# The last forty LSTM steps: kept input parts copied into PSUM by ScalarE, gates in three banks, order by hand

## The chip, the cores and the metric

One core of a Trainium2 chip runs the whole layer. The metric is the device time of one execution in microseconds (us), the median of three runs. The engines are named as in the profile: PE is TensorE's matmuls, PEld its weight loads, ACT is ScalarE, DVE is VectorE, POOL is GpSimd, SP the queue that issues DMAs.

## The reference, cut to what matters

A graph layer (6250 nodes, 256 features, 100000 edges) adds a gather-and-sum network and a linear attention block to x. Its result goes through a layer norm and then an LSTM over all 6250 nodes as one sequence, a gate by argmax and weighted prefix and suffix sums. The change is in the LSTM:

```python
x_proj = einsum('btd,gd->btg', x, W_ih) + b_ih + b_hh
def step(carry, xp):
    h, c = carry
    gates = xp + h @ W_hh.T
    i, f, g, o = split(gates, 4)
    c = sigmoid(f) * c + sigmoid(i) * tanh(g)
    h = sigmoid(o) * tanh(c)
...
logits = lstm_out @ W_lin.T + b_lin
w = argmax(logits) * lstm_out          # two classes: 0 or 1
inc = cumsum(w)
return 2 * lstm_out + (inc - w) * fw_att + (inc[-1] - inc) * bw_att
```

## The kernel before, in words

The sequence of 6250 is cut into NC = 125 pieces of NS = 50 nodes, which run side by side: one column per piece. A piece needs the state at the end of the piece before it. The kernel gets it by a warm-up: every piece first runs its own last WARM = 40 steps from a zero state, and the state reached is handed to the next piece as its beginning (line 984). Then all 50 steps run for good. At the end the final states are compared with those that had been handed on, to a tolerance of 2^-20 (lines 1011 to 1023); only if one differs by more does a loop node by node run instead (line 1028 on). So the loop at line 980 has 90 steps: 40 warm ones (s = 10 to 49), then s = 0 to 49.

State and gates lie with features on the partitions: h and c are two halves (a = 0, 1) of 128 partitions x 125 columns, and each half's four gates are four blocks of 125 columns in one PSUM bank. A step (`step`, line 938) adds W_hh's products onto banks that already hold the inputs' products: for each half a, gate g and half k of h one matmul, 16 in all (line 945). Then, half by half, ACT makes the four gates with the bias in the instruction (line 954), DVE i*g, f*c and their sum c (lines 960 to 962), ACT tanh(c) (line 964) and DVE h (line 965). While that runs, PE brings the inputs of the next step into the other pair of banks.

There are two ways in which they come. In the warm steps and for s = 0 to 9, `inputs` (line 905) multiplies the normed rows by W_ih: 16 matmuls (line 912). In the warm steps `store` (line 917) also copies these banks to SBUF, bank 0 by ACT (line 920) and bank 1 by DVE (line 921), and sends them to HBM (line 922). In the last forty steps, whose inputs are the same as in the warm ones, `fetch` (line 924) gets them back, two steps ahead of use, and `inputs_again` (line 929) puts them into PSUM by one matmul of 500 columns with the identity for each half (line 933). In these steps the products of h go by k first (`by_half`), so that the first eight need only h's first half.

Beside the steps run `residual`, `normed`, `columns` and `kept`, which prepare the normed rows of later steps, and `gated` (line 832) for the step before: two matmuls of h with w_d give the difference of the logits on all partitions (line 835), DVE masks h with it into w (line 837), adds w to inc (line 842), and adds w and inc to h, each with a weight per feature, half by half (line 845): four instructions. `gated` writes h in place, so it comes after the products that read it.

The order on each engine is set by a scheduler at compile time, from the program's order and the dependencies; two instructions on one PSUM bank of a tile are kept in order.

Of the kernel before, what the change touches and what calls it, by code (L numbers as in the profile page):

```python
# [26 lines left out]

NC, NS = 125, 50
HEADS, HC = 8, 32
KD = D // P  # L30
# [23 lines left out]
BANK = 512  # L54
# [6 lines left out]
WARM = 40  # L61
# [15 lines left out]
def gps_layer(ctx: ExitStack, tc: tile.TileContext, x, src, dst, cols, rows, kvln, wqkv, mw1, mw2, gw1, gw2,  # L77
              wih, whh, blstm, out):
    nc = tc.nc
# [4 lines left out]
    x_d = dram.tile([WARM * P, KD * 4 * NC], F32, name="x_d")  # L84


    ident = big.tile([P, P], F32, name="ident")
# [79 lines left out]
    with ExitStack() as s1:  # L167
# [535 lines left out]
        with tc.manual_schedule(engines={mybir.EngineType.PE, mybir.EngineType.DVE, mybir.EngineType.Activation}):  # L703
# [3 lines left out]
            while slot < GROUPS - COUNTED or running or before or any(s >= slot for s in starts):  # L707
                g = slot + COUNTED
# [91 lines left out]
    def block(g, a):  # L800
        return slice((g * KD + a) * P, (g * KD + a + 1) * P)
# [3 lines left out]

    begin_h = wl.tile([P, KD, NC], F32, name="begin_h")
    begin_c = wl.tile([P, KD, NC], F32, name="begin_c")
    c = wl.tile([P, KD, NC], F32, name="c")

# [12 lines left out]
    for k in range(KD):  # L822
        d = wl.tile([P, 1], F32, name="wlin_d")
        nc.vector.tensor_sub(d, col("wlin", 2 * k + 1), col("wlin", 2 * k))
        nc.vector.tensor_scalar(w_d[:, k, :], ones, d, None, op0=ALU.mult)
    one_r = ones[:, :NC]
    inc = wl.tile([P, KD, NC], F32, name="inc")
    rest = wl.tile([P, KD, NC], F32, name="rest")
    rest_t = wl.tile([P, D], F32, name="rest_t")

    def gated(s, pool, pl):

        h_s = hs[:, :, s * NC:(s + 1) * NC]
        for k in range(KD):
            nc.tensor.matmul(pl, w_d[:, k, :], h_s[:, k, :], start=(k == 0), stop=(k == KD - 1))
        w = pool.tile([P, KD, NC], F32, name="w")
        nc.vector.scalar_tensor_tensor(w, pl[:, None, :].to_broadcast([P, KD, NC]), thr, h_s, op0=ALU.is_gt,
                                       op1=ALU.mult)
        if s == 0:
            nc.vector.tensor_copy(inc, w)  # L840
        else:
            nc.vector.tensor_add(inc, inc, w)
        for i, t in ((0, w), (2, inc)):
            for k in range(KD):
                nc.vector.scalar_tensor_tensor(h_s[:, k, :], t[:, k, :], half[:, i, k:k + 1], h_s[:, k, :],
                                               op0=ALU.mult, op1=ALU.add)

    def others(pool, pt):

        for k in range(KD):  # L850
            sums_k = pool.tile([P, NC], F32, name="sums_k")
            nc.vector.tensor_tensor_scan(sums_k, one_r, inc[:, k, :], 0.0, op0=ALU.mult, op1=ALU.add)
            every = pool.tile([P, 1], F32, name="every")
            nc.vector.tensor_mul(every, sums_k[:, NC - 1:NC], half[:, 1, k:k + 1])
            nc.vector.tensor_sub(sums_k, sums_k, inc[:, k, :])
            nc.vector.tensor_scalar(rest[:, k, :], sums_k, half[:, 2, k:k + 1], every, op0=ALU.mult, op1=ALU.add)
            nc.tensor.transpose(pt[:NC, k * P:(k + 1) * P], rest[:, k, :], ident)
        nc.vector.tensor_scalar(rest_t[:NC], pt[:NC], 2.0, None, op0=ALU.mult)

    with tc.tile_pool(name="lstm", bufs=2) as rp, tc.tile_pool(name="ps3", bufs=4, space=PSUM) as ps, \  # L860
            tc.tile_pool(name="ps_y", bufs=2, space=PSUM) as ps_y:

        AHEAD, FETCH = 3, 2

        def residual(s):

# [50 lines left out]
        def store(s, banks):  # L917

            t = rp.tile([P, KD, 4 * NC], F32, name="x_out", bufs=1)
            nc.scalar.copy(t[:, 0, :], banks[0].rearrange("p g c -> p (g c)"))  # L920
            nc.vector.tensor_copy(t[:, 1, :], banks[1].rearrange("p g c -> p (g c)"))
            nc.sync.dma_start(x_d[(s - NS + WARM) * P:(s - NS + WARM + 1) * P, :], t.rearrange("p k m -> p (k m)"))

        def fetch(s):
            t = rp.tile([P, KD, 4 * NC], F32, name="x_in", bufs=FETCH)
            nc.sync.dma_start(t.rearrange("p k m -> p (k m)"), x_d[(s - NS + WARM) * P:(s - NS + WARM + 1) * P, :])
            return t

        def inputs_again(t):
            banks = []  # L930
            for a in range(KD):
                pg = ps.tile([P, 4, NC], F32, name="pg")
                nc.tensor.matmul(pg.rearrange("p g c -> p (g c)"), ident, t[:, a, :], start=True, stop=False,
                                 skip_group_check=True)
                banks.append(pg)
            return banks

        def step(banks, h, put, by_half):


            if h is not None:
                parts = [(k, a) for a in range(KD) for k in range(KD)]
                for k, a in sorted(parts) if by_half else parts:
                    for g in (I, G, F, O):
                        nc.tensor.matmul(banks[a][:, SLOT[g], :], w_hh[:, k, block(g, a)], h[:, k, :], start=False,  # L945
                                         stop=(k == KD - 1), skip_group_check=True)
            for a in range(KD):
                pg = banks[a]
                gate = {}
                for g in (I, G, F, O):  # L950
                    if g == F and h is None:
                        continue
                    gate[g] = rp.tile([P, NC], F32, name=f"gate{g}")
                    nc.scalar.activation(gate[g], pg[:, SLOT[g], :], AF.Tanh if g == G else AF.Sigmoid,  # L954
                                         bias=bias(g, a))
                if h is None:
                    nc.vector.tensor_mul(c[:, a, :], gate[I], gate[G])
                else:
                    new = rp.tile([P, NC], F32, name="new")
                    nc.vector.tensor_mul(new, gate[I], gate[G])  # L960
                    nc.vector.tensor_mul(gate[F], gate[F], c[:, a, :])
                    nc.vector.tensor_add(c[:, a, :], gate[F], new)
                t_c = rp.tile([P, NC], F32, name="t_c")
                nc.scalar.activation(t_c, c[:, a, :], AF.Tanh)
                nc.vector.tensor_mul(put(a), gate[O], t_c)

        order = [(s, True) for s in range(NS - WARM, NS)] + [(s, False) for s in range(NS)]
        minus_half = rp.tile([P, 1], F32, name="minus_half", bufs=1)
        nc.vector.memset(minus_half, -0.5)
        fresh = iter([s for s, _ in order if s >= NS - WARM][:WARM] + list(range(NS - WARM)))  # L970
        first = [residual(next(fresh)) for _ in range(AHEAD)]
        first = [normed(*r) for r in first]
        for r in first:
# [2 lines left out]
        h = None  # L976
        banks = inputs(order[0][0])
        store(order[0][0], banks)
        fetched = {}
        for i, (s, warm) in enumerate(order):  # L980
            if s == 0:
                for t, of in ((begin_h, h), (begin_c, c)):
# [1 line left out]
                    nc.vector.tensor_copy(t[:, :, 1:], of[:, :, :NC - 1])  # L984
                nc.vector.tensor_copy(c, begin_c)
                h = begin_h
            now = rp.tile([P, KD, NC], F32, name="h_w") if warm else hs[:, :, s * NC:(s + 1) * NC]
            step(banks, h, lambda a: now[:, a, :], not warm and s >= NS - WARM)
            for t in at_columns:
                kept(*t)  # L990
            ready = [normed(*t) for t in at_residual]
            if i + 1 < len(order):
                s_next, warm_next = order[i + 1]
                if s_next in fetched:
                    banks = inputs_again(fetched.pop(s_next))
                else:
                    banks = inputs(s_next)
                    if warm_next:
                        store(s_next, banks)
            s_far, warm_far = order[min(i + 1 + FETCH, len(order) - 1)]  # L1000
            if not warm_far and s_far >= NS - WARM and i + 1 + FETCH < len(order):
                fetched[s_far] = fetch(s_far)
# [4 lines left out]
            at_residual = [residual(s) for s in islice(fresh, 2 if i % 5 == 4 else 1)]  # L1007
            h = now


        agree = rp.tile([P, 1], F32, name="agree", bufs=1)
        parts = rp.tile([P, 2], F32, name="parts", bufs=1)
        for i, (end, begin) in enumerate(((h, begin_h), (c, begin_c))):
            d = rp.tile([P, KD, NC - 1], F32, name="d")
# [3 lines left out]
            nc.vector.reduce_sum(parts[:, i:i + 1], d.rearrange("p k c -> p (k c)"), axis=AX.X)  # L1018
        nc.vector.tensor_add(agree, parts[:, 0:1], parts[:, 1:2])
        pa = ps.tile([P, BANK], F32, name="pg")  # L1020
# [3 lines left out]
        gated(NS - 1, rp, ps_y.tile([P, D], F32, name="pm")[:, :NC])  # L1024
        others(rp, ps_y.tile([P, D], F32, name="pm"))
# [128 lines left out]
```

## Time and profile before

| | |
|---|---|
| median of 3 runs | 1652.07 us (1650.72 to 1653.43) |
| the profiled execution | 1649.37 us, span 1646.5 us, mean granted clock of TensorE 0.958 |
| PE busy over the span | 1498.1 us (91%) |
| DVE, ACT, POOL | 947.2 (58%), 611.7 (37%), 695.2 (42%) |
| gather, attention and graph network | to about 960 us |
| warm steps | x_out first at 964.3, last at 1287.6 us |
| last forty steps | first identity matmul at 1368.3, last at 1591.4 us |
| after them | agreement, weighted sums, output, to 1646.5 us |

A stretch of the warm steps, by the same columns as elsewhere in the document (stretch, length, then busy time and number of instructions of PE, PEld, DVE, ACT and POOL, granted clock, DMA share, GB/s):

```profile
1200.00:1300.00 100.00, 100.00 (x847) 100.00 (x846) 57.63 (x221) 49.49 (x158) 7.60 (x14) 1.00 0.14 58
```

How to read it: a float32 matmul shows as two records on PE, each with a weight load. A timeline line gives the start, the length of a run of like instructions, the engine, the line of the kernel, output and inputs, shapes and the number; in brackets stands how long the engine had been idle and what ended that. In lines of groups the number after the bar is the busy time in us and the mean duration in ns, and after the second bar the idle time before them.

### The profile page before, as it was taken

Reading aid. Unit: us, or ns where it says so; the run is one execution under the profiler, and the core shown is the slowest. Engines: PE = TensorE matmul, PEld = TensorE weight load, DVE = VectorE, ACT = ScalarE, POOL = GpSimd, SP = SyncE. Lnnn points to the kernel's source line nnn. Section 1 sums busy time; section 2 is a strip of 40 time slices with the busy share of each in tenths; the row PEclk is TensorE's granted clock in tenths of the full one; section 3 lists DMA queues with packets and bytes.
Section 4 is the critical chain, followed back from the end, with each engine's and each line's share of the span. In section 5 each row is a group of like instructions: output and inputs, shape, how many; then the busy total and the mean of one; then the engine's idle time right before and its main releaser. Section 6 shows DMA issues by size and latency. Waiting matters only on the chain. (4 is left out here: it accounts for less than half of the span.)

```text
span 1646.5 us, 30983 instructions
## 1 busy us (share of the span) xinstructions
PE 1498.1 (91%) x11312; PEld 1398.0 (85%) x11312; DVE 947.2 (58%) x3028; ACT 611.7 (37%) x1866; POOL 695.2 (42%) x713
## 2 busy tenths in 40 slices
PE   1688899899989969999999889999999999999985
PEld 1477788888889969998999879999999998888864
DVE  6878778888842212222222285555555556777777
ACT  2553323433311114333332244555554434444440
POOL 0277777777777747777777400000000000000005
PEclk9689989999989979999999989999999999999996
DMA  9533333333346683333333321111111001333214
GB/s 243 188 89 98 102 101 100 100 100 99 101 142 177 172 196 103 104 106 105 104 106 105 117 74 65 54 60 64 63 64 64 26 1 63 96 94 88 88 51 157
DMA packets 57708, 166.00 MB, mean 101 GB/s; under 512 B 13040, under 2 KB 21879, under 8 KB 55669
## 3 DMA queue, kind: packets, MB, share of 16 engines
q0 software_dynamic: 31008, 84.71, 18.2%
q1 hardware_dynamic: 22884, 75.07, 14.2%
q10 hardware_dynamic: 3652, 4.11, 1.1%
q8 instruction: 93, 1.52, 0.4%
q14 instruction: 71, 0.58, 0.1%
HBM read 130.56 MB, written 33.28 MB: 100 GB/s over the span
## 5 line engine op out<-in xcount | busy, mean ns | idle before, releaser
L380 POOL DMA_INDIRECT eg<-xn_d,si x646 | 643.5, 996 | 220.3 <-issue 99.0
L401 PE MATMUL pg<-here,eg 128*128 128x96 f32 x2584 | 399.5, 281 | 54.7 <-DMA eg<-xn_d,si 40.5
L401 PEld LDWEIGHTS pg<-here,eg 128*128 128x128 f32 x2584 | 363.9, 198 | 86.3 <-DMA eg<-xn_d,si 43.3
L954 ACT ACTIVATE gate<-pg,b_l 128x125 f32<-128x125 f32 x718 | 201.8, 366 | 229.7 <-PE pg L945 228.4
L411 DVE TENSOR_TENSOR sums<-sums,pg 128x192 f32 x162 | 57.4, 354 | 381.9 <-PE pg L401 200.5
L912 PE MATMUL pg<-yT,w_ih 128*128 128x125 f32 x1600 | 186.9, 275 | 0.0
L945 PE MATMUL pg<-sums,w_hh 128*128 128x125 f32 x1568 | 183.1, 275 | 0.0
L912 PEld LDWEIGHTS pg<-yT,w_ih 128*128 128x128 f32 x1600 | 182.7, 192 | 0.1
L945 PEld LDWEIGHTS pg<-sums,w_hh 128*128 128x128 f32 x1568 | 179.0, 192 | 0.0
L881 POOL TENSOR_TENSOR ln_r<-ln_v,minus_half 125x1 f32<-125x1 f32 x50 | 27.4, 552 | 343.1 <-DVE ln_v L879 314.5
L1083 POOL TENSOR_TENSOR xr<-xr,rest_t 125x1024 f32<-125x1024 f32 x8 | 22.9, 2898 | 312.3 <-DVEq L1028 312.3
L945 PE MATMUL pg<-h_w,w_hh 128*128 128x125 f32 x1248 | 146.0, 276 | 0.2 <-ACT x_out L920 0.2
L945 PEld LDWEIGHTS pg<-h_w,w_hh 128*128 128x128 f32 x1248 | 143.1, 192 | 0.6 <-ACT x_out L920 0.4
L620 ACT ACTIVATE sums<-mm,vec 128x125 f32<-128x125 f32 x100 | 36.5, 365 | 269.5 <-DVE sums L411 178.8
L604 PE MATMUL mm<-sums,g 128*128 128x125 f32 x800 | 119.1, 285 | 1.8 <-DVE counts L643 1.6
L615 PE MATMUL mm<-z,g 128*128 128x125 f32 x800 | 114.7, 284 | 1.0 <-ACT z L610 1.0
L604 PEld LDWEIGHTS mm<-sums,g 128*128 128x128 f32 x800 | 106.6, 198 | 5.3 <-issue 1.8
L455 PE MATMUL mm<-m,xnT 128*125 128x256 f32 x400 | 107.9, 394 | 0.6 <-DVE counts L643 0.5
L615 PEld LDWEIGHTS mm<-z,g 128*128 128x128 f32 x800 | 102.0, 196 | 1.1 <-ACT z L610 1.1
L463 ACT ACTIVATE mm<-kv 125x512 f32<-125x512 f32 x50 | 30.1, 602 | 190.7 <-DVE kv L460 190.7
L610 ACT ACTIVATE z<-mm,vec 128x125 f32<-128x125 f32 x200 | 56.3, 367 | 91.5 <-PE mm L604 91.5
L391 DVE TENSOR_TENSOR here<-iota,drel 128x384 f32<-128x384 f32 x162 | 89.3, 551 | 0.0
(239 smaller groups left out, 2162.6 us busy)
## 6 DMA issues: line engine op xcount, KB each, us to landing
x_d<-x_out SPq DMA_DIRECT2D x40, 500.0 KB
x_in<-x_d SPq DMA_DIRECT2D x40, 500.0 KB
xr<-in_x_dram SPq DMA_DIRECT2D x10, 1120.0 KB
eg<-xn_d,si POOLq DMA_INDIRECT x646, 2.8
counts<-xn_d SPq DMA_DIRECT2D x16, 384.0 KB
xn_d<-xn SPq DMA_DIRECT2D x5, 1120.0 KB
out_dram<-o SPq DMA_DIRECT2D x12, 448.0 KB
xr<-in_x_dram SPq DMA_DIRECT2D x10, 130.0 KB
```

Source lines behind the costliest of these rows:

```text
L380: nc.gpsimd.indirect_dma_start(out=g, out_offset=None, in_=xn_d[:], in_offset=bass.IndirectOffsetOnAxis(ap=at, axis=0))
L391: nc.vector.tensor_tensor(here[:, :n, :], iota[:, None, :W].to_broadcast([P, n, W]), drel[:, gi * GT:gi * GT + n, None].to_broadcast([P, n ...
L401: nc.tensor.matmul(pg[:, k, :], g[:, k * P:(k + 1) * P], here[:, i, :], start=(i == 0 and k == 0), stop=(i == n - 1), skip_group_check=True)
L411: nc.vector.tensor_add(window, window, pg)
L455: nc.tensor.matmul(pkv[:r, at], xnT[:, k, j * NC:(j + 1) * NC], w_qkv[:, k, D:][:, at], start=(k == 0 and half == 0), stop=(k == KD - 1), ...
L604: nc.tensor.matmul(p1[:, m, :], g1[:, k, m * P:(m + 1) * P], sums[:, k, at], start=(m == 0 and k == 0), stop=(k == KD - 1), skip_group_che ...
L610: nc.scalar.activation(z1[:, m, :], p1[:, m, :], AF.Relu, bias=col("gb1", m))
L615: nc.tensor.matmul(p2[:, a, :], g2[:, m, a * P:(a + 1) * P], z1[:, m, :], start=(a == 0 and m == 0), stop=(m == 2 * KD - 1), skip_group_ch ...
L620: nc.scalar.activation(sums[:, a, at], p2[:, a, :], AF.Identity, bias=col("gb2", a))
L912: nc.tensor.matmul(pg[:, SLOT[g], :], w_ih[:, k, block(g, a)], yT[:, k, s * NC:(s + 1) * NC], start=(i == 0 and k == 0), stop=False, skip_ ...
L945: nc.tensor.matmul(banks[a][:, SLOT[g], :], w_hh[:, k, block(g, a)], h[:, k, :], start=False, stop=(k == KD - 1), skip_group_check=True)
L954: nc.scalar.activation(gate[g], pg[:, SLOT[g], :], AF.Tanh if g == G else AF.Sigmoid, bias=bias(g, a))
```

## The change

The loop of 90 steps becomes one of 50 (40 warm, then s = 0 to 9). The last forty steps are written out as a part of their own, in an order by hand for PE, DVE and ACT (`manual_schedule`):

- The kept inputs have the biases in them: `store` writes bank + bias, both halves by a DVE add.
- The gates of a step lie in three banks: i, f, o of half 0, the same of half 1, and g of both halves. There are two sets of three.
- The kept inputs of the next step come into the other set by three ScalarE copies (250, 375 and 375 columns). For steps 10 and 11 the identity matmuls do it.
- One tanh makes g of both halves, one sigmoid makes i, f and o of a half, without a bias in the instruction. tanh(g) and c lie side by side (`gc`), so that i*g and f*c are one multiply.
- `gated` is taken apart: logits right behind the step's products on PE, and on DVE the mask, the sum and the weighting by inc behind h; the weighting by w goes into the next step, before each half of h.
- Three fetched inputs are kept instead of two.

In the steps before, the four gates are now one tile, and `new` is made in place. The diff, cut to its core:

```diff
-    c = wl.tile([P, KD, NC], F32, name="c")
+    gc = wl.tile([P, KD, 2, NC], F32, name="gc")
+    c = gc[:, :, 1, :]
+    b_s = wl.tile([P, KD, 4], F32, name="b_s")
+    for g in range(4):
+        nc.vector.tensor_copy(b_s[:, :, SLOT[g]], b_l[:, g * KD:(g + 1) * KD])
...
+    def logits(s, pl):
         for k in range(KD):
-            nc.tensor.matmul(pl, w_d[:, k, :], h_s[:, k, :], start=(k == 0), stop=(k == KD - 1))
+            nc.tensor.matmul(pl, w_d[:, k, :], of_step(s)[:, k, :], start=(k == 0), stop=(k == KD - 1))
+
+    def weighted(s, i, of, k):
+        h_k = of_step(s)[:, k, :]
+        nc.vector.scalar_tensor_tensor(h_k, of[:, k, :], half[:, i, k:k + 1], h_k, op0=ALU.mult, op1=ALU.add)
+
+    def summed(s, pool, pl):
...
+        for k in range(KD):
+            weighted(s, 2, inc, k)
+        return w
...
-        AHEAD, FETCH = 3, 2
+        AHEAD, FETCH = 3, 3
...
-            nc.scalar.copy(t[:, 0, :], banks[0].rearrange("p g c -> p (g c)"))
-            nc.vector.tensor_copy(t[:, 1, :], banks[1].rearrange("p g c -> p (g c)"))
+            for a in range(KD):
+                nc.vector.tensor_tensor(t[:, a, :].rearrange("p (g c) -> p g c", g=4), banks[a],
+                                        b_s[:, a, :, None].to_broadcast([P, 4, NC]), op=ALU.add)
...
-        order = [(s, True) for s in range(NS - WARM, NS)] + [(s, False) for s in range(NS)]
+        KEPT = NS - WARM
+        order = [(s, True) for s in range(KEPT, NS)] + [(s, False) for s in range(KEPT)]
...
+        sets = [([ps.tile([P, 3, NC], F32, name=f"pg{i}{a}") for a in range(KD)], ps.tile([P, KD, NC], F32, name=f"pg_g{i}"))
+                for i in range(2)]
+
+        def into_banks(s, t):
+            others_a, g_b = sets[s % 2]
+            parts = [(g_b, t[:, :, SLOT[G], :])] + [(others_a[a], t[:, a, :SLOT[G], :]) for a in range(KD)]
+            if s < KEPT + 2:
+                return [partial(nc.tensor.matmul, to, ident, of, start=True, stop=False, skip_group_check=True)
+                        for to, of in parts]
+            return [partial(nc.scalar.copy, to, of) for to, of in parts]
...
+        with tc.manual_schedule(engines={mybir.EngineType.PE, mybir.EngineType.DVE, mybir.EngineType.Activation}):
+            for bring in into_banks(KEPT, fetched.pop(0)):
+                bring()
+            fetched.append(fetch(KEPT + FETCH))
+            w = None
+            for s in range(KEPT, NS):
+                more = into_banks(s + 1, fetched.pop(0)) if s + 1 < NS else []
+                for k, a_ifo in ((0, 0), (1, 0), (0, 1), (1, 1)):
+                    gates = [(I, a_ifo), (F, a_ifo), (O, a_ifo)]
+                    for g, a in gates if a_ifo else [(G, a) for a in range(KD)] + gates:
+                        product(s, g, a, k)
+                pl = ps_y.tile([P, BANK], F32, name="pl")[:, :NC]
+                logits(s - 1, pl)
+                others_a, g_b = sets[s % 2]
+                nc.scalar.activation(gc[:, :, 0, :], g_b, AF.Tanh)
+                for a in range(KD):
+                    gates = rp.tile([P, 4, NC], F32, name="gates")[:, :SLOT[G], :]
+                    nc.scalar.activation(gates, others_a[a], AF.Sigmoid)
+                    for bring in more[a:a + 1]:
+                        bring()
+                    two = rp.tile([P, 2, NC], F32, name="two", tag="h_w")
+                    nc.vector.tensor_mul(two, gates[:, :2, :], gc[:, a])
+                    nc.vector.tensor_add(c[:, a, :], two[:, 0, :], two[:, 1, :])
+                    t_c = rp.tile([P, NC], F32, name="t_c")
+                    nc.scalar.activation(t_c, c[:, a, :], AF.Tanh)
+                    if w is not None:
+                        weighted(s - 2, 0, w, a)
+                    nc.vector.tensor_mul(of_step(s)[:, a, :], gates[:, SLOT[O], :], t_c)
+                for bring in more[KD:]:
+                    bring()
+                w = summed(s - 1, rp, pl)
+                if s + 1 + FETCH < NS:
+                    fetched.append(fetch(s + 1 + FETCH))
+            for k in range(KD):
+                weighted(NS - 2, 0, w, k)
```

More of the change, by code (lines that the diff above doesn't have):

```diff
@@ L829, in gps_layer, with of_step @@
     rest_t = wl.tile([P, D], F32, name="rest_t")
-    def gated(s, pool, pl):
-        h_s = hs[:, :, s * NC:(s + 1) * NC]
+    def of_step(s):
+        return hs[:, :, s * NC:(s + 1) * NC]
+    def logits(s, pl):
         for k in range(KD):
-            nc.tensor.matmul(pl, w_d[:, k, :], h_s[:, k, :], start=(k == 0), stop=(k == KD - 1))
+            nc.tensor.matmul(pl, w_d[:, k, :], of_step(s)[:, k, :], start=(k == 0), stop=(k == KD - 1))
[3 more added lines that the diff above has]
+    def summed(s, pool, pl):
         w = pool.tile([P, KD, NC], F32, name="w")
-        nc.vector.scalar_tensor_tensor(w, pl[:, None, :].to_broadcast([P, KD, NC]), thr, h_s, op0=ALU.is_gt,
+        nc.vector.scalar_tensor_tensor(w, pl[:, None, :].to_broadcast([P, KD, NC]), thr, of_step(s), op0=ALU.is_gt,
                                        op1=ALU.mult)
@@ L842, in gated @@
             nc.vector.tensor_add(inc, inc, w)
[L843 to L846, printed above, removed]
+        for k in range(KD):
+            weighted(s, 2, inc, k)
+        return w
+    def gated(s, pool, pl):
+        logits(s, pl)
+        w = summed(s, pool, pl)
+        for k in range(KD):
+            weighted(s, 0, w, k)
     def others(pool, pt):
         for k in range(KD):
-            sums_k = pool.tile([P, NC], F32, name="sums_k")
+            sums_k = pool.tile([P, NC], F32, name="sums_k", tag="t_c")
             nc.vector.tensor_tensor_scan(sums_k, one_r, inc[:, k, :], 0.0, op0=ALU.mult, op1=ALU.add)
@@ L858, in others @@
         nc.vector.tensor_scalar(rest_t[:NC], pt[:NC], 2.0, None, op0=ALU.mult)
-    with tc.tile_pool(name="lstm", bufs=2) as rp, tc.tile_pool(name="ps3", bufs=4, space=PSUM) as ps, \
-            tc.tile_pool(name="ps_y", bufs=2, space=PSUM) as ps_y:
-        AHEAD, FETCH = 3, 2
+    with tc.tile_pool(name="lstm", bufs=2) as rp:
+        AHEAD, FETCH = 3, 3
+        s2 = ExitStack()
+        ps = s2.enter_context(tc.tile_pool(name="ps3", bufs=4, space=PSUM))
+        ps_y = s2.enter_context(tc.tile_pool(name="ps_y", bufs=2, space=PSUM))
         def residual(s):
@@ L924, in fetch @@
         def fetch(s):
-            t = rp.tile([P, KD, 4 * NC], F32, name="x_in", bufs=FETCH)
-            nc.sync.dma_start(t.rearrange("p k m -> p (k m)"), x_d[(s - NS + WARM) * P:(s - NS + WARM + 1) * P, :])
-            return t
[L929 to L936, printed above, removed]
@@ L938, in step @@
-        def step(banks, h, put, by_half):
-            if h is not None:
[L942 to L946, printed above, removed]
+            t = rp.tile([P, KD, 4, NC], F32, name="x_in", bufs=FETCH)
@@ new lines, in fetch, with step @@
+            nc.sync.dma_start(t.rearrange("p k g c -> p (k g c)"), x_d[(s - NS + WARM) * P:(s - NS + WARM + 1) * P, :])
+            return t
+        def step(banks, h, put):
+            if h is not None:
+                for a in range(KD):
+                    for k in range(KD):
+                        for g in (I, G, F, O):
+                            nc.tensor.matmul(banks[a][:, SLOT[g], :], w_hh[:, k, block(g, a)], h[:, k, :], start=False,
+                                             stop=(k == KD - 1), skip_group_check=True)
@@ L947, in step @@
             for a in range(KD):
                 pg = banks[a]
-                gate = {}
+                gates = rp.tile([P, 4, NC], F32, name="gates")
+                gate = {g: gates[:, SLOT[g], :] for g in range(4)}
                 for g in (I, G, F, O):
@@ L952, in step @@
                         continue
-                    gate[g] = rp.tile([P, NC], F32, name=f"gate{g}")
                     nc.scalar.activation(gate[g], pg[:, SLOT[g], :], AF.Tanh if g == G else AF.Sigmoid,
@@ L958, in step @@
                 else:
-                    new = rp.tile([P, NC], F32, name="new")
+                    new = gate[I]
                     nc.vector.tensor_mul(new, gate[I], gate[G])
@@ L965, in step @@
                 nc.vector.tensor_mul(put(a), gate[O], t_c)
-        order = [(s, True) for s in range(NS - WARM, NS)] + [(s, False) for s in range(NS)]
+        KEPT = NS - WARM
+        order = [(s, True) for s in range(KEPT, NS)] + [(s, False) for s in range(KEPT)]
         minus_half = rp.tile([P, 1], F32, name="minus_half", bufs=1)
         nc.vector.memset(minus_half, -0.5)
-        fresh = iter([s for s, _ in order if s >= NS - WARM][:WARM] + list(range(NS - WARM)))
+        fresh = iter([s for s, _ in order])
         first = [residual(next(fresh)) for _ in range(AHEAD)]
@@ L978, in gps_layer @@
         store(order[0][0], banks)
-        fetched = {}
+        fetched = []
         for i, (s, warm) in enumerate(order):
@@ L986, in gps_layer @@
                 h = begin_h
-            now = rp.tile([P, KD, NC], F32, name="h_w") if warm else hs[:, :, s * NC:(s + 1) * NC]
-            step(banks, h, lambda a: now[:, a, :], not warm and s >= NS - WARM)
+            now = rp.tile([P, KD, NC], F32, name="h_w", tag="h_w") if warm else of_step(s)
+            step(banks, h, lambda a: now[:, a, :])
             for t in at_columns:
@@ L993, in gps_layer @@
                 s_next, warm_next = order[i + 1]
[L994 to L1002, printed above, removed]
+                banks = inputs(s_next)
+                if warm_next:
+                    store(s_next, banks)
+            if KEPT - FETCH <= s < KEPT and not warm:
+                fetched.append(fetch(s + FETCH))
             if not warm and s > 0:
@@ L1008, in gps_layer @@
             h = now
+        s2.close()
+        s2 = ExitStack()
+        ps = s2.enter_context(tc.tile_pool(name="ps_k", bufs=1, space=PSUM))
+        ps_y = s2.enter_context(tc.tile_pool(name="ps_l", bufs=2, space=PSUM))
+        sets = [([ps.tile([P, 3, NC], F32, name=f"pg{i}{a}") for a in range(KD)], ps.tile([P, KD, NC], F32, name=f"pg_g{i}"))
[7 more added lines that the diff above has]
+            return [partial(nc.scalar.copy, to, of) for to, of in parts]
@@ new lines, in product @@
+        def product(s, g, a, k):
+            others_a, g_b = sets[s % 2]
+            to = g_b[:, a, :] if g == G else others_a[a][:, SLOT[g], :]
+            nc.tensor.matmul(to, w_hh[:, k, block(g, a)], of_step(s - 1)[:, k, :], start=False, stop=(k == KD - 1),
+                             skip_group_check=True)
+        with tc.manual_schedule(engines={mybir.EngineType.PE, mybir.EngineType.DVE, mybir.EngineType.Activation}):
[11 more added lines that the diff above has]
+                logits(s - 1, pl)
+                others_a, g_b = sets[s % 2]
+                nc.scalar.activation(gc[:, :, 0, :], g_b, AF.Tanh)
+                for a in range(KD):
+                    gates = rp.tile([P, 4, NC], F32, name="gates")[:, :SLOT[G], :]
[15 more added lines that the diff above has]
+                    fetched.append(fetch(s + 1 + FETCH))
+            for k in range(KD):
+                weighted(NS - 2, 0, w, k)
@@ L1011, in gps_layer @@
+        h = of_step(NS - 1)
         agree = rp.tile([P, 1], F32, name="agree", bufs=1)
@@ L1013, in gps_layer @@
         for i, (end, begin) in enumerate(((h, begin_h), (c, begin_c))):
-            d = rp.tile([P, KD, NC - 1], F32, name="d")
+            d = rp.tile([P, KD, NC], F32, name="d", tag="h_w")[:, :, :NC - 1]
             nc.vector.tensor_sub(d, end[:, :, :NC - 1], begin[:, :, 1:])
@@ L1017, in gps_layer @@
             nc.vector.tensor_scalar(d, d, TOL * TOL, None, op0=ALU.is_le)
-            nc.vector.reduce_sum(parts[:, i:i + 1], d.rearrange("p k c -> p (k c)"), axis=AX.X)
+            nc.vector.tensor_reduce(parts[:, i:i + 1], d, axis=AX.XY, op=ALU.add)
         nc.vector.tensor_add(agree, parts[:, 0:1], parts[:, 1:2])
-        pa = ps.tile([P, BANK], F32, name="pg")
+        pa = ps_y.tile([P, BANK], F32, name="pl")
         nc.tensor.matmul(pa[:1, :1], agree, ones[:, 0:1], start=True, stop=True)
@@ L1023, in gps_layer @@
         nc.vector.tensor_copy(agreed, pa[:1, :1])
-        gated(NS - 1, rp, ps_y.tile([P, D], F32, name="pm")[:, :NC])
-        others(rp, ps_y.tile([P, D], F32, name="pm"))
+        gated(NS - 1, rp, ps_y.tile([P, BANK], F32, name="pl")[:, :NC])
+        others(rp, ps_y.tile([P, BANK], F32, name="pl")[:, :D])
+        s2.close()
     right = nc.values_load(agreed[0:1, 0:1], min_val=0, max_val=2 * D * (NC - 1))
```

## The prediction

> **What bounds the kernel now.** I read first the table of busy time by stretch, to find the change's stage: the last forty steps run from the first product of step 10 (1370.51 us) to the end of the state at 1599.4.
>
> ```profile
> core 0: us, PE busy (x) PEld busy (x) DVE busy (x) ACT busy (x) POOL busy (x), PEclk, DMA share, GB/s
> 1375.00:1592.00 217.00, 217.00 (x1523) 182.00 (x1522) 155.87 (x534) 104.77 (x383) 0.00 (x0) 1.00 0.29 89
> ```
>
> PE never pauses there, at full clock; DVE is at 72%, ACT at 48%, DMA at 0.29. Matmul ends are modelled, so I took starts from the timeline of one step:
>
> ```profile
> 1404.25 0.61 PE L835 MATMUL pm<-sums,w_d 128*128 128x125 f32 x4
> 1404.69 3.74 PE L945 MATMUL pg<-sums,w_hh 128*128 128x125 f32 x32
> 1404.86 0.31 ACT L964 ACTIVATE t_c<-c 128x125 f32<-128x125 f32 x1 [0.48 <-DVE c L962]
> 1405.20 0.29 DVE L965 TENSOR_TENSOR sums<-gate,t_c 128x125 f32<-128x125 f32 x1 [0.43 <-ACT t_c L964]
> ...
> 1407.63 1.64 ACT L954 ACTIVATE gate<-pg,b_l 128x125 f32<-128x125 f32 x6 [2.47 <-PE pg L945]
> ...
> 1408.27 1.84 PE L933 MATMUL pg<-x_in,ident 128*128 128x500 f32 x4
> 1408.29 0.29 DVE L960 TENSOR_TENSOR new<-gate,gate 128x125 f32<-128x125 f32 x1 [0.92 <-ACT gate L954]
> ...
> 1409.95 0.61 PE L835 MATMUL pm<-sums,w_d 128*128 128x125 f32 x4
> ...
> 1410.39 3.74 PE L945 MATMUL pg<-sums,w_hh 128*128 128x125 f32 x32
> ```
>
> A step is 5.70 us (1404.69 to 1410.39; over 39 steps, 1370.51 to 1592.68, 5.697). PE's stream fills it: w_hh products 3.58 (32 records at 0.112; a matmul is two records, 0.224), identity matmuls that bring the kept inputs 1.68, logits 0.44. Meanwhile h's second half ends at 1405.49 and its products are not due before 1406.5: the chain through ACT and DVE hides behind PE. So **PE is the bound, and the chain has about 1 us in hand**.
>
> **Removed.** The identity matmuls leave 38 of the 40 steps (10 and 11 keep them): PE's work falls to 3.58 + 0.44 = 4.02 us. Were PE still the bound, 38 x 1.68 = 64 us would go. But the chain h -> products -> gates -> c -> h was covered by that 1.68 us, so what is late next must be added up. In the new order the chain is shorter in places: the three sigmoids of a half are one instruction, both tanh(g) another, i*g and f*c one multiply of 250.
>
> **Prices.** Rows of before for the new shapes:
>
> ```profile
> L903 ACT COPY yT<-pt 128x250 f32<-128x250 f32 x50 | 17.7, 368 | 42.8 <-PE pt L899 42.8
> L920 ACT COPY x_out<-pg 128x500 f32<-128x500 f32 x40 | 22.6, 564 | 0.7 <-ACT gate L954 0.5 <-DMA x_d<-x_out 0.2
> L463 ACT ACTIVATE mm<-kv 125x512 f32<-125x512 f32 x50 | 30.1, 602 | 190.7 <-DVE kv L460 190.7
> L842 DVE TENSOR_TENSOR inc<-inc,w 128x250 f32<-128x250 f32 x49 | 20.6, 420 | 1.6
> ```
>
> A sigmoid of 375 columns out of PSUM lies halfway between the first two, 0.47 us; the multiply of 250 is 0.42. The seed copies go from SBUF to PSUM as line 463 does (0.602 at 512); falling with the slope between the first two rows, 0.78 ns a column, a copy of 375 is 0.50 and one of 250 is 0.40.
> Handovers: PE to ACT 0.25 (bank 0's 24 records end at 1404.69 + 2.69 = 1407.38, the gate starts at 1407.63); ACT to DVE 0.03 (t_c ends 1405.17, next at 1405.20); DVE to DVE, dependent, 0.03; DVE to ACT 0.09 (c ends 1404.76, t_c 1404.86). DVE to PE is hidden in this stage, and shows only in the last step:
>
> ```profile
> 1597.65 0.28 DVE L965 TENSOR_TENSOR sums<-gate,t_c 128x125 f32<-128x125 f32 x1
> ...
> 1598.08 0.46 PE L835 MATMUL pm<-sums,w_d 128*128 128x125 f32 x2 [1.21 <-DVE sums L965]
> ```
>
> 0.15 here, 0.05 at the next such pair, where h's second half ends at 1599.39 and PE starts at 1599.44; I take 0.12.
>
> **The new loop**, from the first product that needs h's second half (k=1), in us:
> 1. five matmuls (g of both halves, i, f, o of half 0): 1.12
> 2. PE to ACT 0.25, sigmoid of half 0 0.47: 1.84
> 3. handover and multiply 0.03 + 0.42, add 0.03 + 0.29: 2.61
> 4. tanh(c) of half 0 starts 0.09 later at 2.70; ACT takes the next instruction 0.21 behind it (as t_c at 1201.48, x_out at 1201.70), so the sigmoid of half 1 starts at 2.91
> 5. (its products end at 11 x 0.224 = 2.46, plus 0.25 = 2.71: 0.20 earlier, no bound)
> 6. sigmoid 0.47, multiply 0.45, add 0.32, handover 0.09: 4.24
> 7. tanh(c) 0.31, handover 0.03, h 0.29, DVE to PE 0.12: **4.99**
>
> h's first half is there at about 3.45; the five k=0 matmuls (1.12) end at 4.57, before 4.99. PE idles about 1 us a step in two gaps; the loop is a pure chain.
> **Beside it.** ACT: the seed copies (0.40, 0.50, 0.50) stand between the sigmoid and tanh(c) of each half, and behind the last tanh. They stand in front of tanh(c), which h waits for; but ACT waits 1.84 to 2.70 and 3.38 to 4.24 there anyway, so a copy costs nothing until it passes 0.86; beyond that, every ns is a ns per step. ACT sums to 3.3 us a step. DVE: the weighting of w moves into the waits for tanh(c) (0.34 from 2.55, h is due at 3.04); behind h, the masked product, the sum and two weightings last to 1.35 of the next step, and the next multiply is due at 1.87: 0.5 in hand. DVE sums to 4.25 us, the nearest rival bound. Its masked product waits for logits, which PE ends at 2.90.
> SP: the fetch of step s+4 waits for the copies of s+1, and has two steps, over 10 us, to land; in before a fetch had less than 12 us and nothing waited for it. Same bytes.
>
> **Once.** Step 10 has step 11's identity matmuls: no gain. At the boundary PSUM is handed to new tiles and the hand-written part begins: between 0 and 3 us, as PE has 0.44 + 1.68 to do while the chain of step 9 (about 2.7) ends; I take 1. At the end DVE stands behind one more masked product, sum and weightings: before, they were fitted into gaps at 1597 to 1599.3, now they follow h in written order: +1.5.
> **The 40 warm steps.** Storing becomes two DVE adds of 500 (0.68 each, the row of line 460 at 512: 0.683) in place of an ACT copy (0.56) and a DVE copy (0.68). DVE gains 0.68 a step where it was at 57%. Cover: h is complete at 1210.35 and PE comes to its products at 1213.05, after the input products, transposes and residual; 2.7 us in hand against 0.68. I take 0; without that cover it would be 40 x 0.68 = 27 us. The gate tiles and four small bias copies: nothing.
>
> **Sum.** 39 x (5.70 - 4.99) = 27.7, less 1 and 1.5: 25 us. Profiled execution 1649.37 (span 1646.5) to about 1624; the median shown is 2.7 above it: 1652.1 - 25 = **1627**.
>
> **A rule against the change.** The Trainium skill, "TensorE: Matmul & The Clock Gate", section "HAM oscillation", says the clock halves only after idle gaps over some 3.4 us. Mine are 0.6 and 0.4: full clock, 4.99 a step. The trace is less kind:
>
> ```profile
> 130.00:140.00 10.00, 7.80 (x52) 6.28 (x50) 9.23 (x28) 2.92 (x8) 7.87 (x8) 0.98 0.34 101
> 140.00:150.00 10.00, 10.00 (x55) 9.44 (x55) 7.99 (x21) 3.48 (x11) 7.76 (x8) 0.68 0.33 93
> ```
>
> In the gather stage no gap in the first stretch is over 0.93, yet the granted clock then falls to 0.68 (0.57 at 230 to 240). But starts there are thin (52 records in 10 us); the new loop has 36 in 4.99, 72 in 10 us, and PE works 80% of it. I take the full clock. At 0.57 the step is PE's 36 x 0.196 = 7.1 us.
>
> **Rivals.**
> - **Clock falls (slower), 8%.** For: the row above. Against: the density; 100 to 130 held 66 to 68 records with clocks of 0.90 to 1.00. Products of half 1 then set the loop: 22 records at p + 0.25 + 2.08 from the sigmoid on; it reaches 5.70 at p = 0.153, a clock of 0.73. Below that the change loses. A slow step fills PE again, so it would alternate: half the steps at 7.1, half at 5.0, mean 6.05: 1652 + 14 + 2.5, about 1668.
> - **The chain is longer, 16%.** DVE with 0.5 in hand, ACT's copies or handovers under two waits: 5.3 a step, 1652 - 15.6 + 2.5 = 1639. For: four engines in strict order with small slacks. Against: each is over 0.2.
> - **Shorter, 8%.** ACT instructions overlap by 0.11, DVE to PE 0.05, sigmoid at the copy's slope from a lower base: 4.75, 1652 - 37 + 2.5 = 1617. PE's 4.02 (about 1589) is out of the chain's reach.
> - **Eaten elsewhere, 5%.** The warm steps' 27 us come onto the path, or the boundary waits: 1652.
> - **Not what it says, 1%.** The Trainium skill's page "PSUM — Partial Sum Buffer", "Summary: rules for kernel authors", wants ACT-written seeds to be 0, since such writes do not mark a word as written (no row here shows it). Here PE writes each bank first (steps 10, 11), which marks it, and no later matmul there starts a group. If inputs were lost, the end states would disagree and the one-by-one path run: 6250 steps of over 1.5 us, above 10 ms. Rounding alone does not do it: c near 1 rounds at 1.2e-7, the tolerance is 9.5e-7.
>
> **Numbers.** Forecast 62%, its own range 1619 to 1636 (steps of 4.8 to 5.2). The range reaches to the shorter and the longer chain: 1613 to 1646. What can be told from no change is 0.2%, 3.3 us. Faster 0.87, same 0.04, slower 0.09.
>
> **What would show it.** Right: a step of 5.0 us; PE waiting for DVE's h twice a step; no 500-column matmuls after step 11; copies inside ACT's waits; clock 1.00; warm steps still 8.2 us. Wrong: DVE without idle, tanh(c) waiting for a copy, a clock under 0.8, or warm steps over 8.3.

## The result, and the profile after

| | before | after |
|---|---|---|
| median on the same chip | 1651.53 us (1650.72 to 1653.43) | 1627.52 us (1626.88 to 1627.92) |
| ratio, 95% interval | | 0.9853 [0.984, 0.9866] |
| profiled execution, span | 1649.37, 1646.5 | 1627.92, 1626.1 |
| one of the last steps | 5.70 | 4.945 |

The step is measured from one tanh(g) to the next, since all 40 of them wait for PE: step 10's starts at 1377.5, step 49's at 1571.1; less step 10's own 5.70 (it still brings inputs by the identity), (193.6 - 5.70)/38 = 4.945 us.

Busy time by stretch of the kernel after, columns as before: the warm steps and the new steps.

```profile
1200.00:1300.00 100.00, 100.00 (x850) 100.00 (x849) 64.19 (x233) 44.89 (x147) 7.60 (x14) 1.00 0.16 63
1390.00:1570.00 180.00, 165.44 (x1312) 151.72 (x1310) 143.40 (x439) 104.60 (x293) 0.00 (x0) 1.00 0.32 98
```

PE is no longer full in the second row, and nothing else is: DVE 80%, ACT 58%. PE's records say it more plainly than its modelled busy time: 36 a step at 0.112 are 4.03 of 4.945 us. Where no engine is full, a chain of instructions that wait for one another is to be looked for. The waits say which one it is (kernel after, 1385 to 1560 us, 35 steps; engine and line that waited, what it waited for, sum in us, number, longest; waits under 0.15 us are left out):

```profile
ACT t_c L1072 <- DVE gc L1070: 35.2, 72, 0.6
ACT gc L1061 <- PE pg_g L1044: 28.4, 35, 0.8
PEld pg_g L1044 <- DVE sums L1075: 27.6, 71, 0.5
DVE two L1069 <- ACT gates L1064: 19.6, 35, 0.6
```

It is a ring: PE waits for h twice a step (71 times), ACT for PE, DVE for the sigmoid of half 0, ACT for c twice a step (72 times). No row has a copy (lines 1066 and 1077) as what was waited for. One turn of the ring, from the first product of k = 1 to the next, in the timeline of after:

```profile
1451.70 0.52 PEld L1044 LDWEIGHTS pg_g<-sums,w_hh 128*128 128x128 f32 x4 [0.29 <-DVE sums L1075]
1451.70 0.71 PE L1044 MATMUL pg_g<-sums,w_hh 128*128 128x125 f32 x4
...
1453.17 0.48 ACT L1064 ACTIVATE gates<-pg 128x375 f32<-128x375 f32 x1 [0.29 <-PE pg L1044]
1453.55 0.38 ACT L1066 COPY pg_g<-x_in 128x250 f32<-128x250 f32 x1
1453.69 0.42 DVE L1069 TENSOR_TENSOR two<-gates,gc 128x250 f32<-128x250 f32 x1 [0.56 <-ACT gates L1064]
1454.14 0.29 DVE L1070 TENSOR_TENSOR gc<-two 128x125 f32<-128x125 f32 x1
...
1454.47 0.31 ACT L1072 ACTIVATE t_c<-gc 128x125 f32<-128x125 f32 x1 [0.54 <-DVE gc L1070]
1454.68 0.46 ACT L1064 ACTIVATE gates<-pg 128x375 f32<-128x375 f32 x1
1454.81 0.29 DVE L1075 TENSOR_TENSOR sums<-gates,t_c 128x125 f32<-128x125 f32 x1
1455.04 0.47 ACT L1066 COPY pg<-x_in 128x375 f32<-128x375 f32 x1
...
1455.18 0.42 DVE L1069 TENSOR_TENSOR two<-gates,gc 128x250 f32<-128x250 f32 x1
...
1455.63 0.29 DVE L1070 TENSOR_TENSOR gc<-two 128x125 f32<-128x125 f32 x1
...
1455.95 0.31 ACT L1072 ACTIVATE t_c<-gc 128x125 f32<-128x125 f32 x1 [0.44 <-DVE gc L1070]
...
1456.30 0.29 DVE L1075 TENSOR_TENSOR sums<-gates,t_c 128x125 f32<-128x125 f32 x1
...
1456.64 0.71 PE L1044 MATMUL pg_g<-sums,w_hh 128*128 128x125 f32 x4
```

From start to start: products to sigmoid 1.47; sigmoid to multiply 0.52; to add 0.45; to tanh(c) 0.33; to half 1's sigmoid 0.21; to its multiply 0.50; to add 0.45; to tanh(c) 0.32; to h 0.35; to PE 0.34: together 4.94. The brackets at both tanh(c) are what the copies leave of ACT's waits: 0.54 and 0.44 us.

**Where the time went.** The two profiled executions between like points, after less before, in us (the differences of their start times):

| stretch | difference |
|---|---|
| up to the first LSTM input (961.2 before, 964.0 after; unchanged code) | +2.8 |
| warm steps, up to the product with the handed-over h | +1.2 |
| s = 0 to 9 | 0 |
| boundary, step 9 to step 10 (5.69 and 6.83) | +1.1 |
| 39 steps (222.17 and 193.13) | -29.0 |
| last step, to h (6.71 and 6.37) | -0.3 |
| end of h to the first addition of the transposed rest, lines 1083 and 1159 (11.66 and 14.85) | +3.2 |
| output | +0.6 |
| sum (1646.5 and 1626.1) | -20.4 |

The first row is not the change's doing: that code is the same, and in runs 1 to 8 below it ends between 961.0 and 966.6. The +0.6 at the output has no explanation here. The medians differ by 24.0.

### The profile page after: what moved, and what is told of

Its sections match the earlier page's. It is cut to its first block, busy times and chain, and to the rows that moved or that the text cites. A ratio compares the mean times of both kernels' runs of the same rounds, so it can differ in the third digit from the quotient of the medians.

```text
span 1626.1 us, 30339 instructions
## 1 busy us (share of the span) xinstructions
PE 1462.0 (90%) x11164; PEld 1379.7 (85%) x11164; DVE 964.1 (59%) x2992; ACT 596.7 (37%) x1740; POOL 697.1 (43%) x713
## 5 line engine op out<-in xcount | busy, mean ns | idle before, releaser
L967 ACT ACTIVATE gates<-pg,b_l 128x125 f32<-128x125 f32 x398 | 112.1, 363 | 133.3 <-PE pg L958 115.7
L1044 PE MATMUL pg<-sums,w_hh 128*128 128x125 f32 x960 | 120.3, 275 | 0.0
L1044 PEld LDWEIGHTS pg<-sums,w_hh 128*128 128x128 f32 x960 | 113.6, 192 | 0.0
```

Source lines behind the costliest of these rows:

```text
L1044: nc.tensor.matmul(to, w_hh[:, k, block(g, a)], of_step(s - 1)[:, k, :], start=False, stop=(k == KD - 1), skip_group_check=True)
```

## The experiments

The sum above says what went where in one execution. The rivals ask why: is the loop really the chain, and are the copies and PE's work off it?

**1. All that is new but the copies: identity matmuls in every step.**

```diff
-            if s < KEPT + 2:
+            if s < NS:
```

> The changed kernel with one thing undone: the kept inputs of all forty steps come into PSUM by PE's identity matmuls instead of ScalarE's copies; gates, banks and hand-written order stay. My theory (the chain of 4.94 us was hidden behind 5.70 us of PE work, so all of the gain needs PE's relief): PE has 3.58 + 0.44 + 1.68 = 5.70 us a step again, the step goes back from 4.94 to 5.70, and the time to 1627.5 + 37 x 0.76 = about 1656 us. Rival (the merged gates and the order bring the gain, the copies little): the step stays below 5.2 and the time below 1638 us.

Measured: 1657.12 us (1653.45 to 1660.03), ratio to before 1.0033 [1.0015, 1.0051]; step 5.70. So merged gates, three banks and the hand-written order are worth nothing while PE is full. This run also weighs what the change costs once: at an equal step, warm stores, boundary and end cost 5.4 us (the kernel before took 1651.74 on this chip), of which 2.5 had been foreseen.

**2. Only the copies, in the kernel before** (one gate at a time, two banks, scheduler's order).

```diff
+                if i_again < 2:
                     nc.tensor.matmul(pg.rearrange("p g c -> p (g c)"), ident, t[:, a, :], start=True, stop=False,
                                      skip_group_check=True)
+                else:
+                    nc.scalar.copy(pg.rearrange("p g c -> p (g c)"), t[:, a, :])
```

> The kernel before with one part of the change alone: from step 12 on the kept inputs are copied into PSUM by ScalarE (two copies of 500 columns), with the two banks, eight gate instructions, biases in ScalarE and the scheduler's order as before. My theory (PE is relieved, but the old chain is longer than the new one: a T' loop of eight k=0 products 1.79 us behind h's first half, and DVE's weightings standing in front of h's second half): about 5.5 us a step (5.3 to 5.7), time 1651.5 - 38 x 0.2 = about 1644 us. Rival (the copies alone are the gain): about 4.95 us a step and 1625 us. PE's floor would be 4.02 us.

Measured: 1637.01 us (1636.15 to 1641.07), ratio 0.9923 [0.9903, 0.9943]; step 5.344. The expected chain of 5.5 was 0.16 too long. PE now stops once a step, for the first half of h (timeline of this kernel):

```profile
1452.12 3.84 PE L948 MATMUL pg<-sums,w_hh 128*128 128x125 f32 x32 [1.06 <-DVE sums L968]
```

The copies alone take 0.35 us off each step, and 14.7 us off the time (from 1651.74 on this chip), without what the whole change pays once. The shorter chain then takes another 0.40 off each step (5.344 to 4.945), some 15 us over 38 steps. Less the 5.4 us of run 1, that leaves the 9.5 us between this run and the changed kernel. So the shorter chain is worth nothing while PE is full (run 1), and about half of the gain per step once it is not.

**3. The new steps in the scheduler's order.**

```diff
-        with tc.manual_schedule(engines={mybir.EngineType.PE, mybir.EngineType.DVE, mybir.EngineType.Activation}):
+        with ExitStack():
```

> The changed kernel without the hand-written order for the last forty steps: the scheduler places the same instructions. My theory (the chain is the bound, so what stands in front of its links counts): the scheduler puts three products of half 1 and a logits matmul into PE's second gap in every other step and a seed copy and half 1's sigmoid in front of half 0's tanh(c), which lengthens the chain to about 5.3 us a step (5.1 to 5.5), time about 1641 us. Rival (the order is worth nothing, the three banks and merged gates shorten the chain): 4.94 us and 1627.5 us.

Measured: 1638.37 us (1637.24 to 1638.98), ratio 0.9923 [0.9907, 0.994]; step 5.27 on the mean, and 10.55 for two unlike ones. In one of the two, ACT's timeline in this kernel reads:

```profile
1484.11 0.47 ACT L1066 COPY pg<-x_in 128x375 f32<-128x375 f32 x1
...
1484.52 0.48 ACT L1064 ACTIVATE gates<-pg 128x375 f32<-128x375 f32 x1
...
1485.03 0.48 ACT L1077 COPY pg<-x_in 128x375 f32<-128x375 f32 x1
...
1485.44 0.30 ACT L1072 ACTIVATE t_c<-gc 128x125 f32<-128x125 f32 x1
...
1486.12 0.71 PE L1044 MATMUL pg_g<-sums,w_hh 128*128 128x125 f32 x4 [1.71 <-DVE sums L1075]
```

c is ready at 1485.12 (line 1070 starts at 1484.84 and takes 0.28), but the tanh stands behind half 1's sigmoid and the last copy, and has no bracket: ACT was not idle before it, it was busy with what could wait. PE pays with 1.71 us. So without the order the merged gates and three banks give 0.07 us a step over run 2, and no time; the order is worth 0.33 us a step. The 16% rival of a longer chain (5.3) is what the same instructions do in another order. What merging and banks give singly no run tells.

**4. and 5. Each copy twice, then three times.** The prediction held that a copy costs nothing until it passes ACT's wait of 0.86.

```diff
-            return [partial(nc.scalar.copy, to, of) for to, of in parts]
+            def bring_in(to, of):
+                for _ in range(2):
+                    nc.scalar.copy(to, of)
+
+            return [partial(bring_in, to, of) for to, of in parts]
```

> The changed kernel with every seed copy of ScalarE done twice (the second writes the same values again). My theory (the copies lie in waits of 0.86 us of ScalarE and cost nothing until they pass it): the two copies of 250 end 0.27 us before tanh(c) of half 0 is due, those of 375 0.06 us before tanh(c) of half 1 is due, so the step stays at 4.94 to 4.99 us and the time at 1627.5 to 1629.5 us. Rival (ScalarE's copies are on the chain or ScalarE is the bound): 0.28 + 0.36 + 0.36 = 1.0 us more a step, 1665 us.

> The changed kernel with every seed copy of ScalarE done three times. My theory (the copies are free only up to the end of ScalarE's waits, then every ns counts): with two copies the step was 4.99 us and PE already waited for the seed of i, f, o of half 0; the third such copy (0.36) comes in full before these products and before tanh(c) of half 1, and the third copy of 250 overruns tanh(c) of half 0 by about 0.06: 4.99 + 0.42 = about 5.4 us a step, 1645 us. Rival (a smooth, average load of ScalarE, with slack left): below 5.1 us, 1633 us. Rival (every copy counts): 4.94 + 2.0 = 6.9 us.

Measured: twice 1630.23 us (1628.89 to 1632.24), ratio 0.9871 [0.9855, 0.9888], step 4.992; three times 1654.59 (1652.39 to 1658.96), ratio 1.0022 [1.0014, 1.003], step 5.695. Doubling a step's 1.3 us of copies costs 0.05 us, so the single copies cost nothing that these steps could show. The third cost more than expected, and the size is explained by this line of the run with three:

```profile
1454.60 1.18 ACT L1041 COPY pg_g<-x_in 128x250 f32<-128x250 f32 x3
```

Three copies into one place take 1.18, 0.40 each, where one takes 0.37 to 0.38. The estimate had let each begin 0.11 before the last was done, as ACT does with other successive instructions. Here the second and third begin 0.03 behind the end of the one before: in the trace each of them waits for a semaphore that the copy before it raises. The 375-column ones take 1.48. ACT is then busy 167.37 of 180 us, 5.30 of the step's 5.695: it is nearly full, the step is back at that of the kernel before, and the costs paid once make this version slower than that. Both kinds of delay share in it; the waits of that kernel (1395 to 1560) show both ways in which a copy reaches the ring, past tanh(c) and past PE's products:

```profile
DVE sums L1079 <- ACT t_c L1076: 27.1, 58, 0.6
PEld pg L1048 <- ACT pg L1041: 26.4, 29, 0.9
```

**6. The logits three times: is PE's work off the path?**

```diff
-                logits(s - 1, pl)
+                for _ in range(3):
+                    logits(s - 1, pl)
```

> The changed kernel with the two logits matmuls of a step done three times (same values), 0.88 us more on PE a step. My theory (PE idles 0.46 and 0.28 us in two gaps a step, and pays 0.09 more for the first weight load after each gap): the gaps take it nearly whole, 4.95 to 5.09 us a step, 1628 to 1633.5 us. Rival (PE is still what sets the step): 4.94 + 0.88 = 5.82 us and 1661 us.

Measured: 1627.79 us (1626.4 to 1631.21), ratio 0.9865 [0.9844, 0.9886]; step 4.95. 0.88 us more on PE cost the step nothing. In step 10, which still has the identity matmuls, the same logits come in full: 6.59 us from tanh(g) to tanh(g) instead of 5.70, for there PE is full. In the steps after it PE has 44 records, 4.93 us of work in 4.95: it could take no more.

**7. Shorten the ring at one place: g's products last.** The sigmoid of half 0, not tanh(g), is what the multiply waits for last. With i, f, o of half 0 ahead of g, and the sigmoid ahead of tanh(g), it starts two matmuls (0.45) earlier; tanh(g), 0.39 behind it, then comes last.

```diff
-                    for g, a in gates if a_ifo else [(G, a) for a in range(KD)] + gates:
+                    for g, a in gates if a_ifo else gates + [(G, a) for a in range(KD)]:
...
-                nc.scalar.activation(gc[:, :, 0, :], g_b, AF.Tanh)
...
                     nc.scalar.activation(gates, others_a[a], AF.Sigmoid)
+                    if a == 0:
+                        nc.scalar.activation(gc[:, :, 0, :], g_b, AF.Tanh)
```

> The changed kernel with i, f, o of half 0 ahead of g in PE's order and the sigmoid ahead of tanh(g) in ScalarE's. My theory (the loop runs through the first five k=1 products, the sigmoid, then half 0's multiply): the sigmoid starts two products earlier and the shorter tanh of 250 (0.38 for 0.48) ends the pair, so the multiply starts 0.11 earlier; the products of half 1 (ready at 2.80) do not bound yet: 4.83 to 4.86 us a step, 1623.3 to 1624.5 us. Rival (the loop is set by half 1's products or by VectorE): 4.94 us and 1627.5 us.

Measured: 1624.61 us (1622.53 to 1625.27), ratio 0.9841 [0.9825, 0.9857]; step 4.853 (step 10's own is 5.76 in this order), from which 38 x 0.09 = 3.4 us follow; the medians differ by 2.9, with the kernel before at 1651.05 beside this one and 1651.53 beside the change. Doubled copies and tripled logits move the step by 0.05 or less; two matmuls that only change places on the ring move it by 0.09. That is the evidence that the loop is this ring. A new wait stands in it (timeline of this kernel): half 0's seed is now needed first, and its copy stands behind half 1's sigmoid. The products of k = 0 end late by it: those of k = 1 start at 1452.99, where h's second half is there at 1452.79 and PE could follow at 1452.84. 0.15 are lost.

```profile
1451.78 0.93 PE L1044 MATMUL pg<-sums,w_hh 128*128 128x125 f32 x6 [0.56 <-ACT pg L1067]
```

**8. The last step's logits in the hand-written part, right behind h,** on top of 7 (and `gated` for the last step by its parts).

```diff
+            pl = ps_y.tile([P, BANK], F32, name="pl")[:, :NC]
+            logits(NS - 1, pl)
...
-        gated(NS - 1, rp, ps_y.tile([P, BANK], F32, name="pl")[:, :NC])
+        w = summed(NS - 1, rp, pl)
+        for k in range(KD):
+            weighted(NS - 1, 0, w, k)
```

> As the run before, and the logits of step 49 on PE right behind its h, ahead of the agreement's matmul. My theory (in the changed kernel VectorE stands still 1.0 us at the end for logits that PE holds back behind the agreement): another 1.0 to 1.4 us, 1622 to 1623.4 us. Rival (the wait is hidden behind the branch after it): no difference to the run before.

Measured: 1620.24 us (1618.51 to 1622.32), ratio 0.9815 [0.9798, 0.9832]. From the end of h to the first addition of the transposed rest the profiled execution takes 13.09 us against run 7's 14.76: 1.7 less, a little over the 1.0 to 1.4 expected. The medians differ by 4.4; what is over 1.7 is within the scatter of the stages ahead of the LSTM (5.6), and no gain of this edit.

**9. to 11. The late seed of run 7 taken away:** g first in the products of k = 0, last in those of k = 1, beside run 8 once more. They ran on two other chips, where the kernel before takes 1788.79 us (the first of these runs) and 1790.73 (the other two), so steps compare with the runs above, and times do not. (In the expectations run 8 has the name e5b_g_last_tail, the first of these e5c_g_first_in_front.)

```diff
-                    for g, a in gates if a_ifo else gates + [(G, a) for a in range(KD)]:
+                    gs = [(G, a) for a in range(KD)]
+                    for g, a in gates if a_ifo else (gs + gates if k == 0 else gates + gs):
```

> As e5b_g_last_tail, but the k=0 block has g's two products first again (its seed is copied first, behind the step's last tanh's predecessors), and only the k=1 block has i, f, o of half 0 before g. In e5b the k=0 block began with half 0's gates, whose copy is late, so PE waited 0.56 us for it and the block ended 0.15 us after h's second half was there. If that late block is what keeps the step at 4.855, the step falls to the chain alone: 4.94 less two products' 0.224 x 2 = 0.45 us before the sigmoid, plus tanh(g)'s place in the chain of c, about 4.70 to 4.79; 38 x 0.06 to 0.15 = 2.5 to 6 us less, 1615 to 1618 us. The rival, that the chain through tanh(g) now sets it (g's products end, PE to ACT 0.25, tanh(g) 0.38, multiply), says the step stays at 4.85 and the time at 1620 us.

> e5b_g_last_tail once more, on the same chip as the next run, since e5c_g_first_in_front ran on a chip where the kernel before takes 1789 us. Expected: step 4.855 us, 31 us less than the kernel before on the same chip (1651.5 to 1620.2 in its first run).

> e5c_g_first_in_front once more beside e5b. Its step was 4.81 us in the first run, (188.4 - 5.7)/38, where 4.70 to 4.79 had been expected; 38 x 0.047 = 1.8 us less than e5b on the same chip, if the step is what tells; 0 if the difference is lost at the ends.

Measured: ratios 0.9837 [0.9816, 0.9859] and 0.9829 [0.9804, 0.9853], and run 8's repeat 0.9832 [0.9807, 0.9856]. Side by side the medians are 1760.09 (1757.75 to 1765.01) and 1759.93 (1759.38 to 1768.34). The steps: 4.805, (188.4 - 5.8)/38, against 4.853; 4.70 to 4.79 had been expected. PE's wait for the seed is all but gone (once in 36 steps, in the first of these runs), but of its 0.15 only 0.05 came back: PE now stops for h there, its first weight load stops with it, and the sigmoid starts 1.03 behind the first product of k = 1 (1603.68 and 1604.71) where it was 0.93 in run 7 (1452.99 and 1453.92). The 1.8 us that 0.05 a step should give are lost in a scatter of several us. Which of the two is faster stays open. Both take 28 to 31 us off the time of the kernel before on the same chip, where the change as it was made takes 24.

## Why the prediction was right, step by step

- **PE bound, the chain 1 us in hand, then the ring bound.** Right: runs 1 and 6 hold both halves of it (PE full: the shorter chain is worth nothing; PE not full: more work on it costs nothing).
- **The loop of 4.99.** Right: 4.945, and in part by luck: three terms were off, one up by 0.10, two down by 0.17 together. Step 1 and 2, products and sigmoid, took 1.47 instead of 1.37: the first four records behind a wait last 0.71 (both PE lines of the ring) where four last 0.61 in the stream before (the logits in the prediction's lines), because the first weight load starts with its matmul instead of 0.10 ahead of it: its line in the ring waits for h as well. DVE to ACT took 0.04 instead of 0.09, twice (line 1070 ends 1454.43, line 1072 starts 1454.47), and DVE to PE 0.05 instead of 0.12, so the last step's second row (0.05) was the one to take, not the middle.
- **Copies within ACT's waits.** Right: 0.54 and 0.44 left over; their estimated 0.40 and 0.50 measured 0.37 and 0.47. Runs 4 and 5 show where it ends.
- **DVE 0.5 in hand.** Right for the multiply of half 0, which finds DVE idle for 0.56. At half 1 there is next to nothing in hand: h's first half leaves DVE at 1455.10, the sigmoid ends at 1455.14, the multiply starts at 1455.18. No run adds work to DVE, so how near it is to being the next bound stays open.
- **Boundary +1.** Right: 1.1, as ACT's gates of step 9 release the banks late; the identity matmul behind it (timeline of after):

```profile
1373.90 0.69 PE L1049 MATMUL pg_g<-x_in,ident 128*128 128x250 f32 x2 [0.86 <-ACT gates L967]
```

- **End +1.5.** Mis-sized: 3.2, and 0.6 at the output. The step counted DVE's instructions behind h and no wait. What had been missed stands on PE: the logits of the last step come behind the agreement's product, which waits for nine DVE instructions.

```profile
1579.87 0.19 PE L1096 MATMUL pl<-ones,agree 128*1 128x1 f32 x2 [6.41 <-DVE agree L1094]
1579.99 1.22 PE L842 MATMUL pl<-sums,w_d 128*128 128x125 f32 x4
...
1581.24 0.48 DVE L852 SCALAR_TENSOR_TENSOR w<-pl,thr,sums 128x250 f32<-128x250 f32 x1 [1.00 <-PE pl L842]
```

h was there at 1575.18 (line 1075 of the last step), PE idle, and yet DVE waits 1.00 us for these logits (and 0.37 for the agreement just before). Run 8 puts them behind h, and 1.7 of the 3.2 go; what is left is about the 1.5 that the prediction counted.
- **Warm steps 0.** 1.2 us over 40 steps, 0.03 each: no 27 us, DVE's share rose from 58% to 64% under the same full PE. The same warm steps took between 0.2 and 1.7 us more than before in the other runs, and whether that belongs to the stores was not tried.
- **Clock.** Right: 1.00 from 1390 to 1570, with PE stopping twice a step, for 0.5 us at most. "HAM oscillation" on the Trainium skill's page "TensorE: Matmul & The Clock Gate" warns of idle gaps over about 3.4 us, and these are far below. It does not say that shorter gaps are safe, as the prediction took it; why the gather stage went to 0.68 with pauses under 1 us no run here tells.
- **Not what it says.** Did not come: from the last h (1575.18) to the end of the span (1626.1) are 51 us, and the trace holds no instruction of the loop node by node, so the states reached with copied seeds other than 0 agree with those handed over. (The prediction's 6250 steps of 1.5 us are 9.4 ms, not above 10.) The rule weighed there, of the Trainium skill's page "PSUM — Partial Sum Buffer", "Summary: rules for kernel authors", is stricter than this case, where PE has written each bank first.
- **The sum.** 25 us foreseen, 24.0 measured, by two errors that met: the loop and last step gave 29.4 instead of 27.7 (the last step, counted as a full one of 0.71, gave 0.3), what was paid once was 6.1 in the profile and 5.4 in run 1 instead of 2.5. That the time was right to 1 us is luck; the once-only costs were not right to half.

## What to carry to other kernels

Work taken off a full engine is worth only as much as the chain behind it is short: add that chain up from start to start, waits included, before counting on the removed time; here 64 us of work went and 24 us of time. When a chain is the bound, the order on an engine that is half idle decides: what h waits for must not stand behind what could wait, and copies are free only inside waits that someone has measured. Where code moves into an order of its own, look at both its ends for an instruction that is queued behind another's wait.

## What was not expected of the hardware

- At a stop of PE for h the first weight load waits too, though it reads only W_hh: in the ring PEld and PE both start at 1451.70 and wait for DVE, and four records last 0.71 instead of 0.61. So some 0.1 us goes at each such stop that busy time does not show. The trace puts the wait at the weight load itself; whether the load could go ahead of it no run tells.
- A tanh and the sigmoid behind it start 0.21 apart, with 0.31 of length, so ACT's instructions overlap by 0.10. Successive copies into one PSUM place do not (0.40 and 0.49 each in a row of three), but each waits for a semaphore of the one before; whether they would overlap without it is open.
- On two other chips the kernel before takes 1788.79 and 1790.73 us instead of 1651. Of run 8's kernel the step is 4.85 on either chip, the span 1766.6 and 1619.3: 147.3 us more, and the first tanh(g) starts 147.1 later (1523.5 and 1376.4). All of it lies in what comes before.
